# Sorted rows of an expert layer: loaded by feature blocks and transposed on VectorE, four tiles at a time, in place of TensorE transposes two tiles at a time

## The chip, the core and the metric

The kernel runs on one core of a Trainium2 chip. A core has five engines with instruction queues of their own: PE (TensorE, matmuls; its weight loads are listed as PEld), DVE (VectorE), ACT (ScalarE), POOL (GpSimd) and SP (SyncE, which here only issues DMAs). Sixteen DMA engines move the data that the queues ask for. SBUF is the on-chip memory with 128 partitions, PSUM the memory that PE writes. The metric is device time in microseconds (us) of one execution, the median of several.

## The reference

The input `x` has the shape (4, 32, 128, 128), float32, and goes through two layers.

```
# layer 0, for each of 4 batches: 128 channels-and-phases of a 64x64 image as q (128 x 4096) ... 
energy = einsum('bci,bcj->bij', q, q)            # 4096 x 4096
attn   = softmax(energy / (d_i * d_j), axis=-1)  # d = sqrt of the diagonal
x      = gamma * einsum('bcj,bij->bci', q, attn) + x
# layer 1, on tokens t of 128 features
t = t + linear_attention(layernorm(t))           # 8 heads, K'V form
n = layernorm(t)
p = softmax(n @ router_w + router_b)             # 8 experts
t = t + sum over the two likeliest experts of  p_k / (p_1 + p_2) * (n @ expert_w[k] + expert_b[k])
```

The change lies in the last line: every token goes through two of eight 128x128 expert matrices.

## The kernel before

**The long part.** For each of the four batches, PE computes the 4096 x 4096 energies by blocks of 128 x 512 (`pe`, L609), ACT takes their exponential (`pr`, L612), and PE multiplies that with q (`po`, L497). The energies are symmetric, so only half of them are computed. For the other half DVE transposes each `pr` by 32x32 pieces into a tile `F` (L421); four steps fill one `F`. SP stores `F` to DRAM (`blocks`, L530), waits for that to land, and brings it back with the 32-row groups swapped, in six DMAs (L545). PE then multiplies `F` with q (`pg`, L433), some steps later (`LAG`), ACT sums its rows (L438), and DVE adds the result (`o`, L442). One step is one `pe`, one `po` and one `pg` of 512 columns; a float32 matmul of this kind has two records in the profile.

**The second layer beside it.** For batches 0 to 2 the second layer of a batch runs in the steps of the next batch. It is written as Python generators (`layer1`, `close_rows`, `attention_rows`, `sorted_experts`), and a loop around them advances the generators as the long part goes on, so the order of instructions on PE, DVE, ACT and SP is the order in which the generators yield. Batch 3 comes last, has no long part to hide beside, and computes all experts for all tokens without sorting.

**Sorted experts.** A batch has 32 tiles of 128 tokens, handled in two halves `h`. For a half, `sorted_experts` works out a place for each of its two uses of a token, so that tokens of the same expert lie together and each expert begins at a multiple of 128 rows: `NT` = 39 tiles of 128 rows. A row has `DW` = 132 floats: 128 features and, four times, the factor that the expert's result is multiplied with. POOL scatters the rows from `xn` to the DRAM tensor `xs[h]` with indirect DMAs (L1053). Then come the sorted tiles, in pairs:

- `load` (L1083) brings two tiles from `xs[h]` into one of six buffers inside `xn`, 132 floats a row;
- three pairs later, `products` lets PE transpose the pair (L1124, two 128x128 transposes with the identity), and ACT copies the result from PSUM to SBUF (L1093);
- one pair later PE multiplies each turned tile with its expert's matrix (L1117), whose column in `ew_sb` is read from `begin` into a register (L1109, once for four tiles);
- DVE multiplies the result with the factor, which is column 128 of the loaded rows (L1099), and SP stores it to `ys` (L1103).

`hold` hands out one of three PSUM banks and empties it when `done` is called. Each pair takes two yields. At last POOL gathers the rows of `ys` back by token and adds them (L1165), and SP writes the output (L1159).

**Rows of the next batch.** `close_rows(kc)` ends the first layer for a quarter of a batch. Its `df` tile shares a buffer with the `results` of the sorted experts, and so the quarter kc = 0 waits until the batch before is `sorted`.

Of the kernel before, what the change touches and what calls it, by code (L numbers as in the profile page):

```python
# [12 lines left out]
F32 = mybir.dt.float32  # L13
BF16 = mybir.dt.bfloat16
U32 = mybir.dt.uint32
AF = mybir.ActivationFunctionType
ALU = mybir.AluOpType
# [5 lines left out]
def kernel(  # L23
# [43 lines left out]
    nc = tc.nc  # L67
    P = 128
# [8 lines left out]
    S = 32  # L77
    NH, KQ, D = wk.shape
    E = router_w.shape[1]
# [574 lines left out]
    def layer1(b, st):  # L654
# [76 lines left out]
        def close_rows(kc):  # L731


            def missing():
                return len(st["o"]) < 2 * kc + 2 or any(
                    st["got"][c] < NCH - c - (alone and c == NCH - 1) for c in (2 * kc, 2 * kc + 1)
                )

            late_rows = alone and kc >= 2
            last_rows = alone and kc == 3  # L740

            while "exps" not in st if last_rows else missing():
                yield from idle(1)
            while b > 0 and kc == 0 and not states[b - 1].get("sorted"):
                yield from idle(1)
            den, rd = (stat.tile([P, 2 * NJ], F32, tag=nm, name=f"{nm}_{b}_{kc}") for nm in ("den", "rd"))
            nc.vector.tensor_reduce(den, st["sums"][:, ts(kc, 2 * NJ), :], AX.X, ALU.add)
            nc.vector.reciprocal(rd, den)
            wide = work.tile([P, NJ, 2, 64], F32, tag="grp", name=f"rdx_{b}_{kc}", bufs=2)
            for s in range(2):  # L750
                one = rd[:, ts(s, NJ)][:, :, None]
                nc.vector.tensor_scalar(wide[:, :, s], one.to_broadcast([P, NJ, 64]), gam, None, ALU.mult)
            df = work.tile([P, 8, HW2, 2], F32, tag="df", name=f"df_{b}_{kc}", bufs=1)

            def divide(pb):
                for s in range(2):
                    own = slice(s * 64, s * 64 + 64)
                    o = st["o"][2 * kc + s]
                    for r2 in range(2):
                        rows = slice(r2 * 64, r2 * 64 + 64)  # L760
                        nc.vector.tensor_tensor(  # L761
                            df[own].rearrange("p (a k) (h t) r -> p r a (k h) t", a=4, h=2)[:, r2],
                            o[rows].rearrange("p (a j t) -> p a j t", a=4, t=S),
                            pb[own].rearrange("p (j a t) -> p a j t", a=4, t=S),
                            ALU.mult,
                        )

            yield
            if not last_rows:
                yield  # L770
                yield
            pb, done = hold(f"pbd_{b}_{kc}", divide)
            for j in range(NJ):
                nc.tensor.transpose(pb[:, ts(j, P)], wide[:, j].rearrange("p s c -> p (s c)"), ident)
            yield
            while missing():
                yield from idle(1)
            done()
            if not late_rows:
                yield  # L780
                yield
            tk = T[:, ts(kc, 8), :]
            nc.vector.tensor_tensor(tk, tk, df.rearrange("p k w r -> p k (w r)"), ALU.add)
            bs, stats = batch_stats("a", 8 * kc, 8)
            for j in range(8):
                stats[j]()
                if j == 3:
                    yield
                    yield
            close_stats("a", 8 * kc, 8, bs)  # L790
            yield from idle(1 if late_rows else 3)
            k = 8 * kc
            normalise(range(k, k + 4), rsa, nba)
            if late_rows:
                for j in range(k + 4, k + 8):
                    nc.vector.tensor_scalar(
                        xn[:, j, :D], T[:, j, :], rsa[:, j, :], nba[:, j, :], ALU.mult, ALU.add
                    )
            yield
            if last_rows:  # L800
                keep_running(36)
                done = gram_rows([k + j // 2 + 4 * (j % 2) for j in range(8)])
                yield
                done()
                return
            done = gram_rows(range(k, k + 4))
            yield
            done()
            if not late_rows:
                normalise(range(k + 4, k + 8), rsa, nba)  # L810
            yield
            done = gram_rows(range(k + 4, k + 8))
            yield
            done()
            if alone and kc < 3:
                for g in (2 * kc, 2 * kc + 1):
                    yield
                    done = transpose_rows(g)
                    yield
                    done()  # L820
# [153 lines left out]
        def sorted_experts(h):  # L974
# [98 lines left out]
            yield from idle(3)  # L1073


            bufs = [xn[:, r0 + 2 * i : r0 + 2 * i + 2, :] for i in range(8)]
            pairs = [(g, min(2, NT - 2 * g)) for g in range((NT + 1) // 2)]

            def rows_of(dram_rows, g, n):
                return dram_rows[2 * g * P : (2 * g + n) * P, :].rearrange("(j p) d -> p j d", p=P)  # L1080

            def load(g, n):
                inst = nc.sync.dma_start(bufs[g % 6][:, :n], rows_of(xs[h], g, n))  # L1083
                wait_for(inst.ins, xs_made[h], "a tile holds tokens of any row")
                xs_read[h].append(inst.ins)

            def products(turned, applied):


                def leave(p):  # L1090
                    if turned:
                        g, n = turned
                        nc.scalar.activation(  # L1093
                            bufs[6 + g % 2][:, :n, :D], p[:, : n * P].rearrange("p (j t) -> p j t", t=P), AF.Copy
                        )
                    if applied:
                        g, n = applied
                        result = keep["results"][:, g % 4]
                        nc.vector.tensor_tensor(  # L1099
                            result[:, :n], p[:, 2 * P : 2 * P + n * D].rearrange("p (j c) -> p j c", c=D),  # L1100
                            bufs[g % 6][:, :n, D : D + 1].to_broadcast([P, n, D]), ALU.mult,
                        )
                        nc.sync.dma_start(rows_of(ys, g, n), result[:, :n])  # L1103

                p, done = hold(f"pys_{b}_{h}_{(turned or applied)[0]}", leave)
                if applied:
                    g, n = applied
                    if g % 2 == 0:
                        _, at = nc.values_load_multi_w_load_instructions(  # L1109
                            begin[0:1, h, 2 * g : min(2 * g + 4, NT)], engines=[mybir.EngineType.PE], min_val=0,  # L1110
                            max_val=(E - 1) * D,
                            skip_runtime_bounds_check_because="D times a count of at most E - 1, never negative",
                        )
                        begins[:] = at
                    weights = ew_sb.rearrange("p e c -> p (e c)")
                    for j in range(n):
                        nc.tensor.matmul(  # L1117
                            p[:, 2 * P + j * D : 2 * P + j * D + D], bufs[6 + g % 2][:, j, :D],
                            weights[:, bass.ds(begins[2 * (g % 2) + j], D)], start=True, stop=True,
                        )  # L1120
                if turned:
                    g, n = turned
                    for j in range(n):
                        nc.tensor.transpose(p[:, ts(j, P)], bufs[g % 6][:, j, :D], ident)  # L1124
                return done

            if "results" not in keep:
                keep["results"] = work.tile([P, 4, 2, D], F32, tag="df", name=f"results_{b}", bufs=1)
            done = None
            begins = []  # L1130
            for at in range(len(pairs) + 5):
                if at < len(pairs):
                    load(*pairs[at])
                if done:
                    done()
                yield
                turned, applied = (pairs[at - d] if 0 <= at - d < len(pairs) else None for d in (3, 4))
                done = products(turned, applied) if turned or applied else None
                yield
            if done:  # L1140
                done()
            if h == 1:
                st["sorted"] = True
            yield from idle(1)
# [353 lines left out]
```

## Time and profile before

| what | value |
|---|---|
| median of 3 runs | 1652.24 us (1652.22 to 1652.25) |
| the profiled execution | 1659.2 us, span 1657.4 us |
| granted TensorE clock, mean | 0.996 |
| PE busy | 1623.1 us, 98% |
| DVE busy | 917.4 us, 55% |
| ACT busy | 910.4 us, 55% |
| POOL busy | 596.2 us, 36% |
| DMA packets | 241899, 332.81 MB |
| sorted loads, first and second half of batch 0 | 571 to 636 us, 661 to 719 us |
| of batch 1 | 961 to 1024 us, 1050 to 1107 us |
| of batch 2 | 1332 to 1396 us, 1415 to 1470 us |

The span is the time from the first to the last instruction of the profiled execution; its own time is 1.8 us longer. That execution is 0.4% longer than the median, so differences are compared with differences. A group line of the profile reads: line, engine, operation, tile written and tiles read, shape, number of instructions, busy time, mean nanoseconds of one, and the idle time of the engine before them with what ended it. `SPq` is SP's queue. The sorted stages in the table run from the first to the last sorted load of a half.

### The profile page before, as it was taken

Reading aid. Unit: us, or ns where it says so; the run is one execution under the profiler, and the core shown is the slowest. Engines: PE = TensorE matmul, PEld = TensorE weight load, DVE = VectorE, ACT = ScalarE, POOL = GpSimd, SP = SyncE. Lnnn points to the kernel's source line nnn. Section 1 sums busy time; section 2 is a strip of 40 time slices with the busy share of each in tenths; the row PEclk is TensorE's granted clock in tenths of the full one; section 3 lists DMA queues with packets and bytes.
Section 4 is the critical chain, followed back from the end, with each engine's and each line's share of the span. In section 5 each row is a group of like instructions: output and inputs, shape, how many; then the busy total and the mean of one; then the engine's idle time right before and its main releaser. Section 6 shows DMA issues by size and latency. Waiting matters only on the chain.

```text
span 1657.4 us, 21471 instructions
## 1 busy us (share of the span) xinstructions
PE 1623.1 (98%) x5288; PEld 856.9 (52%) x5288; DVE 917.4 (55%) x2359; ACT 910.4 (55%) x2863; POOL 596.2 (36%) x565
## 2 busy tenths in 40 slices
PE   8999999999999999999999999999999999999987
PEld 5444544455554455555564455555565445554643
DVE  4543353567486443559378453448559533344686
ACT  3555445566575555556575455556657455555376
POOL 1000000001014531456555543346546642436166
PEclk9999999999999999999999999999999999999999
DMA  4555656665349776986778868797668877885001
GB/s 147 199 181 174 198 186 213 230 212 170 131 171 277 246 220 213 271 249 176 207 200 254 265 208 255 214 287 200 167 196 239 277 222 246 240 254 168 15 14 39
DMA packets 241899, 332.81 MB, mean 201 GB/s; under 512 B 31984, under 2 KB 168304, under 8 KB 227440
## 3 DMA queue, kind: packets, MB, share of 16 engines
q1 hardware_dynamic: 207312, 291.92, 55.5%
q0 software_dynamic: 26624, 25.58, 7.5%
q10 hardware_dynamic: 7840, 13.93, 2.8%
q8 instruction: 45, 0.74, 0.2%
q14 instruction: 78, 0.64, 0.1%
HBM read 160.78 MB, written 175.80 MB: 203 GB/s over the span
## 4 chain that ended last, share of the span: by engine, by line
PE 84%; DMA 4%; DVE 4%; SPq 3%; ACT 2%; issue 2%; another core or an unknown queue 1%; POOL 0%; ACTq 0%; DVEq 0%; POOLq 0%
PE po L497 24%; PE pe L609 23%; PE pg L433 20%; PE pys L1117 3%; DMA blocks<-F 3%; PE py L1290 3%; PE pg L453 2%; SPq L545 2%; PE pat L854 2%; PE pys L1124 2%; PE pgram L728 1%; PE ptx L701 1%; DVE df L761 1%; PE pgv L839 0%
## 5 line engine op out<-in xcount | busy, mean ns | idle before, releaser
L612 ACT ACTIVATE pr<-pe 128x512 f32<-128x512 f32 (+1 forms) x576 | 322.4, 560 | 544.0 <-PE pe L609 448.2
L497 PE MATMUL po<-pr,qT 128*128 128x512 f32 (+3 forms) x1152 | 549.6, 559 | 4.2 <-ACT o L502 3.0
L609 PE MATMUL pe<-qn,qn 128*128 128x512 f32 x896 | 459.6, 595 | 2.6 <-ACT pr L612 1.6
L433 PE MATMUL pg<-F,qT 128*128 128x512 f32 x880 | 449.7, 592 | 1.1 <-DMA F<-blocks 1.1
L421 DVE STREAM_TRANSPOSE F<-pr 128x512 f32<-128x512 f32 x440 | 305.9, 702 | 144.8 <-ACT pr L612 127.0
L497 PEld LDWEIGHTS po<-pr,qT 128*128 128x128 f32 x1152 | 215.3, 190 | 251.7 <-issue 221.2
L1165 POOL DMA_INDIRECT acc<-ys,place x128 | 203.2, 1588 | 215.8 <-ACT pr L612 140.3
L438 ACT ACTIVATE junk<-F 128x512 bf16<-128x512 f32 x440 | 273.0, 620 | 1.2 <-DMA F<-blocks 1.2
L433 PEld LDWEIGHTS pg<-F,qT 128*128 128x128 f32 x880 | 166.7, 190 | 195.4 <-issue 181.0
L1053 POOL DMA_INDIRECT xs<-xn,place x192 | 186.0, 969 | 189.7 <-ACT pr L612 116.6
L609 PEld LDWEIGHTS pe<-qn,qn 128*128 128x128 f32 x896 | 155.0, 191 | 115.0 <-issue 104.6
L442 DVE TENSOR_TENSOR o<-o,pg 128x512 f32<-128x512 f32 x110 | 75.3, 684 | 207.9 <-PE pg L433 173.4
L1099 DVE TENSOR_TENSOR results<-pys,xn 128x256 f32<-128x256 f32 x120 | 49.9, 416 | 187.1 <-ACT xn L1093 122.0
L164 POOL TENSOR_TENSOR rn<-ss,neg_half 128x8 f32<-128x8 f32 (+1 forms) x17 | 27.2, 1602 | 320.9 <-DVE ss L296 320.8
L612 ACT ACTIVATION_READ_ACCUMULATOR pr<-pe 128x1 f32 x576 | 112.0, 194 | 0.0
L1093 ACT ACTIVATE xn<-pys 128x256 f32<-128x256 f32 x120 | 45.2, 377 | 112.5 <-PE pys L1124 94.5
L1117 PEld LDWEIGHTS pys<-ew_sb,xn 128*128 128x128 f32 x468 | 70.4, 191 | 53.0 <-issue 49.5
L1165 POOL DMA_INDIRECT yb<-ys,place x64 | 61.8, 965 | 84.5 <-DMA F<-blocks 31.1
L609 PE MATMUL pe<-qn 128*128 128x512 f32 (+3 forms) x256 | 90.2, 435 | 0.7 <-ACT qn L342 0.7
L438 ACT ACTIVATION_READ_ACCUMULATOR junk<-F 128x1 f32 x440 | 84.6, 192 | 0.0
L1117 PE MATMUL pys<-ew_sb,xn 128*128 x468 | 71.7, 275 | 0.4 <-ACT xn L1093 0.4
L164 POOL TENSOR_TENSOR rsa<-dm_a,neg_half 128x8 f32<-128x8 f32 x16 | 28.9, 1807 | 103.1 <-DVE sv_a L688 102.9
(216 smaller groups left out, 1521.1 us busy)
## 6 DMA issues: line engine op xcount, KB each, us to landing
blocks<-F SPq DMA_DIRECT2D x110, 1024.0 KB
F<-blocks SPq DMA_DIRECT2D x220, 192.0 KB
F<-blocks SPq DMA_DIRECT2D x220, 128.0 KB
xn<-xs SPq DMA_DIRECT2D x114, 132.0 KB
ys<-results SPq DMA_DIRECT2D x114, 128.0 KB
F<-blocks SPq DMA_DIRECT2D x220, 64.0 KB
below<-F SPq DMA_DIRECT2D x31, 384.0 KB
T<-in_x_dram SPq DMA_DIRECT2D x64, 128.0 KB
```

Source lines behind the costliest of these rows:

```text
L164: pinned(nc.gpsimd.tensor_tensor(dst, src, neg_half.to_broadcast(list(src.shape)), ALU.pow))
L421: f()
L433: nc.tensor.matmul(pg.rearrange("p (a f) -> p a f", a=4), st["qT"][i][:, ib, :], G[:, :, ib], start=(ib == 0), stop=(ib == NJ - 1),)
L438: nc.scalar.activation(junk, G[:, :, ib], AF.Copy, accum_out=st["sums"][:, NJ * i + ib, jc : jc + 1])
L442: nc.vector.tensor_tensor(st["o"][jc], st["o"][jc], pg, ALU.add)
L497: nc.tensor.matmul(row["po"][:, lo:hi], qT[blk // NJ][:, blk % NJ, :], w, start=start, stop=(row["left"] == 0))
L609: nc.tensor.matmul(pe[:, c0:], qn[jc][:, ts(j, P)], qn[i][:, c0:], start=True, stop=True)
L612: nc.scalar.activation(pr[:, c0:], pe[:, c0:], AF.Exp, accum_out=sums[:, t, i : i + 1]).ins
L1053: inst = nc.gpsimd.indirect_dma_start(xs[h], offset(place[:, i, k : k + 1]), xn[:, k, :], None)
L1099: nc.vector.tensor_tensor(result[:, :n], p[:, 2 * P : 2 * P + n * D].rearrange("p (j c) -> p j c", c=D), bufs[g % 6][:, :n, D : D + 1].to_ ...
L1117: nc.tensor.matmul(p[:, 2 * P + j * D : 2 * P + j * D + D], bufs[6 + g % 2][:, j, :D], weights[:, bass.ds(begins[2 * (g % 2) + j], D)], st ...
L1165: inst = nc.gpsimd.indirect_dma_start(to, None, ys, offset(place[:, i, k : k + 1]), compute_op=op)
```

## The change

Sorted tiles are handled in fours (`quads`, ten for each half, the last with three tiles) and turned without PE and ACT.

- `load` issues four DMAs, one for each block of 32 features. Block `q` goes to partitions 32q to 32q+31: partition 32q+i receives, for each group m of 32 rows, the 32 features of row 32m+i. Each piece is 128 bytes long. The two load buffers, and two for turned tiles, lie in this half's part of `xn`.
- `turn` is one DVE instruction: it transposes every 32x32 piece of the 128x512 tile, which leaves features on partitions and rows along the free axis.
- `product` multiplies four tiles into one PSUM bank; its `leave` multiplies 128x512 at once with `factor` and stores four tiles with one DMA.
- `factor` is a tile of 128x39, loaded once for a half by one DMA that picks column 128 of every row, 4 bytes at a time.
- One quad is loaded every four yields; its turn is due eight yields later, its product eleven, and its result thirteen.
- `close_rows` of all quarters waits until the batch before is `sorted`; a quarter also waits until the quarter two before it has been added, and, before it takes a PSUM bank, until the one before it has.

```diff
-            while b > 0 and kc == 0 and not states[b - 1].get("sorted"):
+            added = st.setdefault("added", set())
+            while b > 0 and not states[b - 1].get("sorted") or kc > 1 and kc - 2 not in added:
                 yield from idle(1)
...
+            while kc > 0 and kc - 1 not in added:
+                yield
             pb, done = hold(f"pbd_{b}_{kc}", divide)
...
             nc.vector.tensor_tensor(tk, tk, df.rearrange("p k w r -> p k (w r)"), ALU.add)
+            added.add(kc)
...
-            bufs = [xn[:, r0 + 2 * i : r0 + 2 * i + 2, :] for i in range(8)]
-            pairs = [(g, min(2, NT - 2 * g)) for g in range((NT + 1) // 2)]
...
-                inst = nc.sync.dma_start(bufs[g % 6][:, :n], rows_of(xs[h], g, n))
...
-                        nc.scalar.activation(
-                            bufs[6 + g % 2][:, :n, :D], p[:, : n * P].rearrange("p (j t) -> p j t", t=P), AF.Copy
-                        )
...
-                        nc.tensor.transpose(p[:, ts(j, P)], bufs[g % 6][:, j, :D], ident)
...
+            room = xn[:, half, :].rearrange("p k w -> p (k w)")
+            parts = [room[:, 4 * DW * i : 4 * DW * i + 4 * D] for i in range(4)]
+            quads = [(g, min(4, NT - 4 * g)) for g in range((NT + 3) // 4)]
+            factor = stat.tile([P, NT, 1], F32, tag="factor", name=f"factor_{b}_{h}")
...
+            def load(g, n):
+                rows = xs[h][4 * g * P : (4 * g + n) * P, :D].rearrange("(m i) w -> i m w", i=S)
+                for q in range(4):
+                    read(
+                        nc.sync.dma_start(
+                            parts[g % 2][ts(q, S), : n * D].rearrange("i (m c) -> i m c", c=S), rows[:, :, ts(q, S)]
+                        )
+                    )
+
+            def turn(g, n):
+                nc.vector.transpose(parts[2 + g % 2][:, : n * D], parts[g % 2][:, : n * D])
+
+            def product(g, n):
 
                 def leave(p):
+                    result = keep["results"][:, ts(g % 2, 4)]
+                    nc.vector.tensor_tensor(
+                        result[:, :n], p[:, : n * D].rearrange("p (j c) -> p j c", c=D),
+                        factor[:, 4 * g : 4 * g + n].to_broadcast([P, n, D]), ALU.mult,
+                    )
...
+                for j in range(n):
+                    nc.tensor.matmul(
+                        p[:, ts(j, D)], parts[2 + g % 2][:, ts(j, D)],
+                        weights[:, bass.ds(begins[j], D)], start=True, stop=True,
+                    )
...
+            read(nc.sync.dma_start(factor, xs[h].rearrange("(t p) w -> p t w", p=P)[:, :, D : D + 1]))
+            leaves = {}
+            for at in range(4 * len(quads) + 10):
+                for first_at, act in ((8, turn), (0, load), (11, product), (13, lambda g, n: leaves.pop(g)())):
+                    if at >= first_at and (at - first_at) % 4 == 0 and (at - first_at) // 4 < len(quads):
...
+                yield
```

## The prediction

> **What bounds the kernel now.** I read the page's busy shares first, then the PE groups with their idle time, the instructions of PE in order of time inside one sorted stage, the DMA share by stage, and last SP's waits.
>
> The page says that PE (TensorE's matmuls) is busy nearly all the time, at an undiminished clock:
>
> ```profile
> span 1657.4 us, 21471 instructions
> PE 1623.1 (98%) x5288; PEld 856.9 (52%) x5288; DVE 917.4 (55%) x2359; ACT 910.4 (55%) x2863; POOL 596.2 (36%) x565
> ...
> PEclk9999999999999999999999999999999999999999
> DMA  4555656665349776986778868797668877885001
> ```
>
> The PE groups show who makes PE wait. The number after the bar is busy time, then the mean of one, then idle time before:
>
> ```profile
> L433 PE MATMUL pg<-F,qT 128*128 128x512 f32 x880 | 449.7, 592 | 1.1 <-DMA F<-blocks 1.1
> L1117 PE MATMUL pys<-ew_sb,xn 128*128 x468 | 71.7, 275 | 0.4 <-ACT xn L1093 0.4
> L1124 PE MATMUL pys<-ident,xn 128*128 128x128 f32 x234 | 45.1, 273 | 0.0
> ```
>
> All idle time before PE instructions adds up to 26 us, most of it at the start and after 1500 us. The reader is to see that in the sorted stages PE works through its list without a hole, so a matmul taken off the list there shortens the run by the room it took, as long as everything that feeds PE keeps pace. That room is not the mean duration. In order of time:
>
> ```profile
> 642.53 0.61 PE L1117 MATMUL pys<-ew_sb,xn 128*128 x4
> 642.98 0.38 PE L1124 MATMUL pys<-ident,xn 128*128 128x128 f32 x2
> 643.20 0.81 PE L609 MATMUL pe<-qn 128*128 128x384 f32 x2
> ```
>
> Two transposes start at 642.98 and the next matmul at 643.20: 0.11 us each. Over all 234 of L1124 the distance to the next start adds up to 25.5 us, 0.109 each.
>
> What feeds PE is the DMA round trip of F (L530 out, L545 back, used by L433). These are the six stages with sorted loads, two for each of batches 0 to 2; the last two numbers are DMA share and GB/s:
>
> ```profile
> 571.00:636.00 65.00, 64.82 (x223) 34.50 (x222) 29.31 (x52) 34.39 (x106) 27.54 (x30) 1.00 0.75 229
> 661.00:719.00 58.00, 58.00 (x215) 32.38 (x214) 27.38 (x52) 30.05 (x93) 28.10 (x18) 1.00 0.95 254
> 961.00:1024.00 63.00, 62.82 (x218) 33.66 (x217) 28.72 (x52) 33.15 (x101) 26.95 (x29) 1.00 0.74 232
> 1050.00:1107.00 57.00, 57.00 (x213) 31.76 (x212) 27.38 (x52) 29.36 (x90) 27.59 (x18) 1.00 0.98 257
> 1332.00:1396.00 64.00, 62.46 (x222) 34.02 (x222) 22.82 (x45) 34.02 (x107) 26.20 (x29) 1.00 0.77 243
> 1415.00:1470.00 55.00, 55.00 (x209) 31.41 (x208) 24.30 (x48) 29.64 (x92) 30.42 (x32) 1.00 0.85 253
> ```
>
> The first stage of a batch leaves the DMA engines a quarter of their time, the second hardly any. The share adds up packet times, which overlap a little: its highest stretch of 10 us anywhere is 1.14, which I take as full. From packet records and PE starts I worked out how early F is back: 9 to 14 us before PE needs it in the first stages, 5 to 11 in the second. That slack is what the change can use up.
>
> **The change, part by part.**
>
> *Transposes off PE.* 117 pairs of tiles, 234 transposes, gone: 234 x 0.109 = 25.5 us. The 468 records of L1117 (two for each of 234 products) and one register load for each four tiles stay. The Trainium skill ("TensorE: Matmul & The Clock Gate", Part 4) gives about 275 ns for a transpose inside a kernel; the mean record here agrees (273 ns), but starts lie 109 ns apart, and by 275 the gain would be 64 us. I go by the distance of starts.
>
> *Copies off ACT.* 120 of L1093, 45.2 us. ACT is 55% busy and mostly waits for PE, so nothing is gained or lost.
>
> *DVE.* 60 turns of 128x512 at L421's 0.70 us add 42 us; 60 multiplies of 128x512 at L442's 0.68 replace 120 of L1099 at 0.416, 41 against 50. Net 33 us, 5.6 in a stage where DVE is busy 23 to 29 of 55 to 65 us. Its idle time covers it; without that, 33 us.
>
> *SP.* 240 loads and 6 factor columns replace 120 loads, 60 stores replace 120: 66 more issues, at 0.43 us 28 us, under 5 a stage. SP is occupied 52 to 73% of the stages, so this fits.
>
> *New waits.* Load g on SP waits for turn g-2 on DVE, listed just ahead of it; behind it queue F's stores and returns. SP already waits there for DVE:
>
> ```profile
> SPq L545 <- DMA blocks<-F: 215.2, 64, 6.1
> SPq L1103 <- DVE results L1099: 79.9, 38, 9.2
> ```
>
> so it is paced by DVE now, and half of the L1103 waits go. A turn waits on DVE for a load listed four steps earlier, some 12 us. Loads now land 1.5 to 6 us after issue, plus 1.3 for three more issues, so it is normally there. Late, it would hold F's transposes (L421) behind it. I cost both at 0 to 2 us a stage, 1 where DMA is tight.
>
> *Order of rows.* close_rows moves one `pbd` by two or three matmuls and one `pgram` past a `pbd`, in batches 1 and 2; the tail of batch 3 has the old order. Nothing.
>
> *DMA, the open price.* Half a batch has 39 tiles. Before: 4992 packets of 528 bytes, taking 9.3 us of 16 engines together (mean 31.9 ns). After: 19968 of 128 bytes, and 4992 of 4 bytes for the factor column. The trace has no 128-byte packet. Its nearest rows, median time of a packet: 9 ns at 4 and 32 bytes, 27 at 512, 84 at 2048, 311 at 8192, which lie on 8.2 ns + 0.037 a byte. That line puts 128 bytes at 13 ns. From below the bound is 9, from above 27, if small reads are served no faster than 512-byte ones. Net per half:
> - 13 ns (factor 9): 16.2 + 2.8 - 9.3 = +9.7 us
> - 15 ns: +12
> - 18 ns for the rows: +16
> - 22 ns for both: 27.5 + 6.9 - 9.3 = +25
> - 27 ns for both: 33.7 + 8.4 - 9.3 = +33
>
> A stage shrinks by 4 us (25.5/6). What does not fit into 1.14 of the rest, beyond a slack of 9 us (first stages) or 5.5 (second), PE waits for. Second stages hold 55.1, 55.9 and 46.8 us of DMA work (share by length) and have room for 61.3, 60.2 and 57.9 (1.14 x 53.8, 52.8, 50.8). At 15 ns the first two overflow by 5.8 and 7.7, so 0.3 + 2.2, rounded up to 3 us of waiting; at 18 by 9.8 and 11.7, so 10.5; at 22 all three, 13.3 + 15.2 + 8.4 = 37. At 27: second stages 21 + 23 + 16, first stages (48.8 + 33 against 69.3, less 9) some 4 each, 73 us. First stages cost nothing up to 22. I take 15 ns, close to the line, with 2 added because the pieces lie 528 bytes apart, at uneven addresses, which no row prices.
>
> The Trainium skill speaks against the change: "DMA: Bandwidth & Descriptors" (Specifications) wants at least 512 bytes for line rate. Read as "128 bytes cost what 512 do", it gives the 27 ns sum below, 1700. No row here settles it.
>
> **Sum.** -25.5 (PE) + 3 (DMA) + 2 (new waits) = -20 us. The profiled execution took 1659.2 us (span 1657.4 and 1.8 around it), 0.4% above the 1652.2 median, so it becomes 1639, and the median 1632.
>
> **Rivals.**
> *A: the DMA engines become the bound (slower).* Mechanism: 128-byte reads cost as much as 512-byte ones, the queue that also carries F fills in the second stages, and L433 waits for F. It decides from about 20 ns on, where the waiting equals 25.5 us. At 22 ns: 1652 - 25.5 + 37 = 1664; at 27: 1652 - 25.5 + 73 = 1700. For it: shares of 0.95 and 0.98, and the one place where DMA backs up today (L433, 1.1 us, at 184 us, as large set-up transfers run) shows that F can arrive late. Against it: the straight line of packet times.
> *B: the wait moves to DVE or SP.* Turns late behind their loads, or the 4992 single elements of the factor column block the queue at the head of a stage. The column takes 2.8 to 8.4 us of the queue a half (9 and 27 ns each). At 2 us of stall in each of six stages 12 us go: 1639; with the column at 8.4, 3 us over the slack in three stages, 21 go: 1648. Against it: the slack, and turns that come 12 us behind their loads.
> *C: the freed room isn't used, no change.* PE would have to wait for ACT or DVE by the same amount; both are half idle, so hardly.
>
> **How the numbers follow.** Forecast (1626 to 1638) 0.42; B 0.11; A 0.44; C 0.03. Forecast and B are faster, A is slower. The range takes the forecast and B whole and A up to 22 to 27 ns: 1626 to 1690, leaving out the dearest part of A and a gain above the 25.5 us. Measurement can tell about 0.2%, 3.3 us. Faster 0.53, same 0.03, slower 0.44.
>
> **What would show it.** Right: L1124 and L1093 gone, PE's busy time near 1598, 128-byte packets at 13 to 15 ns, idle time before L433 a few us, DMA share in second stages about 1.1. Wrong: idle before L433 or L497 of tens of us at 660 to 730 and 1050 to 1120 with releaser F (A), or idle before L421 or the turn released by a load, and SP waiting for turns (B). Wrong in size: PE idle for ACT.

## The result, and the profile after

| kernel | median | ratio to before, 95% interval |
|---|---|---|
| before | 1652.23 us | |
| changed | 1657.99 us (1656.07 to 1660.49, 6 runs) | 1.0041 [1.003, 1.0051] |
| changed, in a later comparison (f0) | 1660.80 us | 1.0054 [1.0038, 1.0071] |

The changed kernel is 0.4 to 0.5% slower, some 7 to 9 us by the ratios, where 20 us of gain were forecast. The chips of the comparisons differ by up to 10 us (the kernel before took 1649.82 on one and 1660.19 on another), so every ratio is to runs of the kernel before on the same chip. For a comparison place by place I use a trace of the unchanged kernel taken with the experiments (e0, span 1651.0 us).

The page of the changed kernel (profiled execution 1658.15 us):

```profile
span 1655.8 us, 20777 instructions
...
PE 1604.1 (97%) x5054; PEld 832.1 (50%) x5054; DVE 944.1 (57%) x2359; ACT 869.0 (52%) x2743; POOL 591.3 (36%) x565
...
DMA  5554756665359898996768789797567999996001
```

PE lost 234 instructions and 19 us of busy time, but the span did not follow. PE waits now, 43.9 us in all against 21.9 in e0. The waits of PE (us in total, times, the longest), in the changed kernel:

```profile
PE pg L433 <- DMA F<-blocks: 7.6, 6, 2.4
PE pgram L728 <- DVE gram L722: 5.7, 2, 2.9
PE pys L1121 <- DVE xn L1099: 5.7, 4, 2.0
```

L433 is F back late, the first line that the forecast watched. The wait of `pys` (the sorted product) begins with a DMA as well; for `gram` that is argued here, and e3 shows it for a part. The groups of DVE (the last columns are idle time and what ended it) show the turn waiting for its load, and the first layer's `df` waiting for a store of the expert results that share its buffer:

```profile
L762 DVE TENSOR_TENSOR df<-o,pbd 64x512 f32<-64x512 f32 x64 | 43.9, 686 | 21.9 <-PE pbd L777 10.8 <-DMA ys<-results 10.4
...
L1099 DVE STREAM_TRANSPOSE xn<-xn 128x512 f32<-128x512 f32 (+1 forms) x60 | 40.6, 677 | 60.2 <-DMA xn<-xs 60.0
```

**Where.** Set matching matmuls of the changed kernel and e0 side by side by their order. The changed kernel is 8.5 us ahead when its PE reaches 667 us (2.9 of them from before any sorted load, so no part of the change), and 0.8 at 767. It gains some 6 until 1064 and loses some 13 until 1167, gains some 6 until 1431 and loses some 5 until 1525. The gains are the first halves and what lies around them. The losses are the second halves and, behind the first two of them, `close_rows`. The first two second halves by windows (length, then busy time of PE, PEld, DVE, ACT, POOL, then granted clock, DMA share, GB/s), first in the changed kernel, then in e0, and last the second window in e2, a variant told below that loads 512-byte pieces and keeps the gain:

```profile
647.00:719.00 72.00, 68.04 (x217) 34.58 (x216) 36.91 (x62) 30.63 (x95) 30.95 (x20) 1.00 0.96 216
1037.00:1111.00 74.00, 69.25 (x214) 34.79 (x213) 37.41 (x62) 30.58 (x95) 29.84 (x20) 0.98 0.94 212
```

```profile
647.00:719.00 72.00, 71.82 (x255) 39.17 (x254) 32.47 (x63) 37.75 (x117) 27.31 (x18) 1.00 0.89 242
1037.00:1111.00 74.00, 73.82 (x264) 40.31 (x263) 32.62 (x62) 38.16 (x119) 29.09 (x19) 1.00 0.89 244
```

```profile
1037.00:1111.00 74.00, 73.23 (x238) 37.79 (x237) 41.75 (x76) 32.41 (x102) 38.17 (x25) 1.00 1.02 264
```

PE idles 4 to 5 us in each window of the changed kernel. Its DMA engines are somewhat busier than in the same windows of e0 (0.96 and 0.94 against 0.89) and move less. But e2 has them at 1.02 and 264 GB/s while PE hardly waits, so it isn't their capacity that ended.

**Each wait costs twice.** PE in order of time at one of the late F, and the granted clock (PEclk) of four stretches behind waits of 2.0 to 2.9 us:

```profile
1084.52 1.02 PE L497 MATMUL po<-pr,qT 128*128 128x512 f32 x2
1087.93 1.10 PE L433 MATMUL pg<-F,qT 128*128 128x512 f32 x2 [2.39 <-DMA F<-blocks]
1088.87 1.84 PE L609 MATMUL pe<-qn,qn 128*128 128x512 f32 x2
1090.50 1.92 PE L497 MATMUL po<-pr,qT 128*128 128x512 f32 x2
1092.21 1.09 PE L433 MATMUL pg<-F,qT 128*128 128x512 f32 x2
```

```profile
761.20:764.60 3.40, 3.40 (x8) 1.80 (x8) 3.31 (x5) 0.99 (x3) 2.91 (x3) 0.51 0.11 22
1088.90:1092.30 3.40, 3.40 (x6) 1.34 (x5) 0.97 (x2) 1.30 (x4) 0.60 (x1) 0.50 1.13 246
1153.80:1160.60 6.80, 5.62 (x13) 3.56 (x14) 6.63 (x13) 1.84 (x6) 5.08 (x4) 0.50 0.46 117
1471.20:1474.60 3.40, 3.40 (x8) 1.72 (x7) 2.96 (x5) 0.69 (x2) 0.00 (x0) 0.50 0.84 242
```

The pairs at 1088.87 and 1090.50 take 1.84 and 1.92 us, and start 1.6 to 1.7 us apart instead of 0.86. Four such stretches, 17 us in all, cost up to 8.5 us on top of the waits. e0 has none between 30 and 1570 us.

**SP.** DMA-issuing instructions don't count as busy, so the page has no line for them. Adding up the durations of all DMA instructions on SP's queue gives 722 us in e0 (1541 of them) and 813 in the changed kernel (1607). In order of time, first the unchanged kernel (e0), then the changed one, each across a few us of batch 0's second half:

```profile
685.95 0.42 SPq L1083 DMA_DIRECT2D xn<-xs  x1
686.47 0.41 SPq L1103 DMA_DIRECT2D ys<-results  x1
686.98 0.42 SPq L1083 DMA_DIRECT2D xn<-xs  x1
687.49 0.49 SPq L1103 DMA_DIRECT2D ys<-results  x1
```

```profile
683.40 2.69 SPq L1093 DMA_DIRECT2D xn<-xs  x4
686.19 1.88 SPq L1109 DMA_DIRECT2D ys<-results  x1
688.17 2.31 SPq L1093 DMA_DIRECT2D xn<-xs  x4
690.58 2.86 SPq L545 DMA_DIRECT2D F<-blocks  x6
693.54 0.38 SPq L1109 DMA_DIRECT2D ys<-results  x1
693.96 0.50 SPq L530 DMA_DIRECT2D blocks<-F  x1
694.56 3.89 SPq L1093 DMA_DIRECT2D xn<-xs  x4
```

The second column is the duration. Four loads hold the queue for 2.3 to 3.9 us, a store behind them for 1.88, and F's return (L545) and store (L530) stand behind both.

How much of F's lateness arises there can be read by matching packet records, in order, to F's stores and returns. In the second halves, from F's fourth transpose (L421) to its landing, 19.3 us pass in e0 and 27.1 in the changed kernel, in the mean. F's time in flight (its store, and its last return, each from issue to landing) did not grow: 7.9 and 7.6 us. All else, time in which F stands in SP's queue, went from 11.3 to 19.5. The largest part of it, from the transpose to the issue of F's store, went from 6.5 to 11.7 us, and the time that SP spends in it issuing other DMAs from 4.3 to 8.4.

### The profile page after: what moved, and what is told of

Read it like the earlier page. It is cut to its first block, busy times and chain, and to the rows that moved or that the text cites. A ratio compares the mean times of both kernels' runs of the same rounds, so it can differ in the third digit from the quotient of the medians.

```text
span 1655.8 us, 20777 instructions
## 1 busy us (share of the span) xinstructions
PE 1604.1 (97%) x5054; PEld 832.1 (50%) x5054; DVE 944.1 (57%) x2359; ACT 869.0 (52%) x2743; POOL 591.3 (36%) x565
## 4 chain that ended last, share of the span: by engine, by line
PE 78%; DMA 8%; DVE 6%; SPq 3%; issue 2%; ACT 2%; POOL 1%; ACTq 0%; DVEq 0%; POOLq 0%
PE po L497 23%; PE pe L609 22%; PE pg L433 19%; PE py L1287 3%; PE pys L1121 2%; PE pg L453 2%; PE pgram L728 2%; PE pat L858 2%; DMA F<-blocks 1%; DMA blocks<-F 1%; DMA acc<-ys,place 1%; DMA xn<-xs 1%; SPq L545 1%; DMA acc<-t 1%; DMA ys<-results 1%
## 5 line engine op out<-in xcount | busy, mean ns | idle before, releaser
L433 PE MATMUL pg<-F,qT 128*128 128x512 f32 x880 | 450.3, 593 | 8.1 <-DMA F<-blocks 7.6
L421 DVE STREAM_TRANSPOSE F<-pr 128x512 f32<-128x512 f32 x440 | 303.8, 698 | 176.4 <-ACT pr L612 166.1
L433 PEld LDWEIGHTS pg<-F,qT 128*128 128x128 f32 x880 | 166.7, 191 | 206.2 <-issue 179.4
L609 PEld LDWEIGHTS pe<-qn,qn 128*128 128x128 f32 x896 | 159.5, 191 | 134.8 <-issue 129.0
L1121 PEld LDWEIGHTS pys<-ew_sb,xn 128*128 128x128 f32 x468 | 61.4, 192 | 32.7 <-issue 23.9
L1099 DVE STREAM_TRANSPOSE xn<-xn 128x512 f32<-128x512 f32 (+1 forms) x60 | 40.6, 677 | 60.2 <-DMA xn<-xs 60.0
L1121 PE MATMUL pys<-ew_sb,xn 128*128 x468 | 62.5, 276 | 5.7 <-DVE xn L1099 5.7
L1287 PE MATMUL py<-ew_sb,xn 128*128 128x512 f32 x128 | 60.2, 610 | 5.1 <-ACT tmp L1244 3.9
```

Of the source, the lines that this page charges most:

```text
L421: f()
L433: nc.tensor.matmul(pg.rearrange("p (a f) -> p a f", a=4), st["qT"][i][:, ib, :], G[:, :, ib], start=(ib == 0), stop=(ib == NJ - 1),)
L609: nc.tensor.matmul(pe[:, c0:], qn[jc][:, ts(j, P)], qn[i][:, c0:], start=True, stop=True)
L1121: nc.tensor.matmul(p[:, ts(j, D)], parts[2 + g % 2][:, ts(j, D)], weights[:, bass.ds(begins[j], D)], start=True, stop=True,)
L1287: nc.tensor.matmul(bank, xn[:, k, :D], ew_sb[:, 4 * h : 4 * h + 4, :], start=True, stop=True)
```

## The experiments

Two theories were left by the comparison. *Pieces*: the many 128-byte packets fill the DMA engines. *Queue*: what SP has to issue fills SP's in-order queue, and F's stores and returns, loads and stores all come late. With them went two smaller suspects, the buffer shared by `df` and `results`, and the factor column.

**e0_before: the kernel before, unchanged.**

> The kernel before, unchanged, profiled again beside the others. Both theories: 1652 us, so a ratio of 1.000 to the runs of before. Its profile tells whether the 7 us by which the first profiled execution (1659.2 us) lay over its median belong to that execution: if the profile lies at 1652 again, the two traces may not be compared by their totals, only place by place.

0.9999 [0.999, 1.0009]. A difference of a tenth of a per cent is about what a comparison leaves open.

**e1_no_turn: what the transposes are worth.** In the kernel before, the transposes and copies are left out, so that the product takes the loaded rows as they are.

```diff
-  p[:, 2 * P + j * D : 2 * P + j * D + D], bufs[6 + g % 2][:, j, :D],
+  p[:, 2 * P + j * D : 2 * P + j * D + D], bufs[g % 6][:, j, :D],
...
-  turned, applied = (pairs[at - d] if 0 <= at - d < len(pairs) else None for d in (3, 4))
+  turned, applied = None, (pairs[at - 4] if 0 <= at - 4 < len(pairs) else None)
```

> The kernel before without its transposes on TensorE and without the copies on ScalarE: the product takes the loaded rows as they are (this part of the computation is left out). Loads, stores and VectorE work are those of before. If the 25.5 us that the prediction gave for the transposes are right, 1627 us (ratio 0.9846). Rival, something else than TensorE's list sets the end of the sorted stages: 1640 us or more.

1631.01 us, 0.9879 [0.9863, 0.9894]: 20 us. PE's 25.5 us are there to be had, less some 4 us more of waiting (idle 25.5 against 21.9).

**e2_wide_rows: the changed kernel with one load for four tiles, in 512-byte pieces.** The turn is issued all the same, but on rows so loaded it doesn't transpose a whole tile; this order of data is what is left out.

```diff
-  for q in range(4): ... parts[g % 2][ts(q, S), : n * D] ... rows[:, :, ts(q, S)]
+  read(nc.sync.dma_start(parts[g % 2][:, : n * D].rearrange("p (j d) -> p j d", d=D),
+      xs[h][4 * g * P : (4 * g + n) * P, :D].rearrange("(j p) d -> p j d", p=P)))
```

> The changed kernel, but each quad is loaded by one DMA with pieces of 512 bytes, row by row, so that the turn on VectorE no longer yields the true transpose (the order of the data is left out). Theory 1, the number of pieces delays F and the stores in the second stages: the waits of TensorE for F vanish, 1637 us or less. Theory 2, the loss comes from close_rows waiting for the last store of the results in the shared buffer: still 1648 us or more. If both hold, between.

1630.13 us, 0.9883 [0.9866, 0.99]. Turns on DVE, products by four, factor column, the new order of `close_rows` and the shared buffer are all in it, and it keeps 19 us of gain. So the loss hangs on how the rows are loaded. PE's and DVE's waits in this kernel:

```profile
PE pg L433 <- DMA F<-blocks: 1.9, 2, 1.1
...
PE pgram L728 <- DVE gram L722: 1.5, 2, 1.0
```

```profile
DVE xn L1098 <- DMA xn<-xs: 21.6, 11, 5.4
```

Even so its second halves have become tight. Between F's landing and PE's need of it, packet records and PE starts of the first two batches leave 1.6 to 5.4 us there (and nothing for one F, at 1075 us), against 5.4 to 10.7 in e0: enough for PE but for that one, and little is left.

**e3_own_results: results of the second half in a free part of `xn`, not in df's buffer**.

```diff
-  result = keep["results"][:, ts(g % 2, 4)]
+  result = results[:, ts(g % 2, 4)]   # h == 1: in xn[:, :HR]
```

> The changed kernel with the results of the second half in a part of xn that is free by then, so that df of the next batch no longer waits for the last stores of the second half. Theory 1 (pieces): no more than 5 us better, 1653 us. Theory 2 (the shared buffer): VectorE no longer waits 4.1 and 6.3 us for the store, TensorE does not wait for gram, and 5.3 + 8.6 = 14 us come back, 1644 us.

1652.18 us, 1.0014 [1.0005, 1.0024], some 4 to 7 us better than the changed kernel (1.0041 and 1.0054). `df` no longer waits for a store (10.4 us before); PE's wait for `gram` goes from 5.7 to 3.4 us. The shared buffer is a part of the loss, not its main cause.

**e4_all_partitions and e5_plain_factor: other forms of the same packets.** e4 gives each of the four loads all 128 partitions and one tile, in 128-byte pieces. e5 reads the factor tile in 156-byte pieces instead of 4992 single elements.

```diff
-  parts[g % 2][ts(q, S), : n * D].rearrange("i (m c) -> i m c", c=S), rows[:, :, ts(q, S)]
+  parts[g % 2][:, : n * D].rearrange("p (q j c) -> p q j c", q=4, c=S)[:, :, j], rows   # e4
-  factor, xs[h].rearrange("(t p) w -> p t w", p=P)[:, :, D : D + 1]
+  factor.rearrange("p t w -> p (t w)"), xs[h][:P, :NT]                                  # e5
```

> The changed kernel with the same number of DMAs and of 128-byte pieces, but each DMA brings one tile to all 128 partitions instead of four tiles to 32 (so the blocks lie in another order and the turn isn't the true transpose). Theory 1a, the number of small pieces costs the time: as the changed kernel, 1658 us. Theory 1b, four DMAs that write to only 32 partitions each are what is slow: near the wide rows' 1630 us.

> The changed kernel, but the factor tile is loaded in pieces of 156 bytes, one for each partition, instead of 4992 pieces of 4 bytes (its values are left out). If the column counts by its packets' time (9 ns each, 2.8 us of 16 engines a half), some 3 us in each second stage come back: 1648 to 1652 us. If single elements are dearer than their records say, more: 1640 us.

e4 1.0066 [1.0052, 1.008], e5 1.0100 [1.0086, 1.0114]. e4 came near its theory 1a, e5 missed both of its numbers. Neither gains: the number of partitions isn't it, nor are the single elements. That e5 is slower than the changed kernel isn't explained. Its profiled run has waits of 10.4 us at 1450 and 7.2 us at 1527 that the changed kernel's traces don't have; e4 and e6, from the same chip, have waits of 4 to 11 us near them too.

**e6_more_time: e2 with four more DMAs per quad, DRAM to DRAM, 128 rows of 512 bytes each.**

```diff
+  for m in range(4):
+      inst = nc.sync.dma_start(spare[g % 2][ts(m, k), :], xs[h][4 * g * P + m * k : 4 * g * P + (m + 1) * k, :D])
```

> The wide rows (1630 us) with four more DMAs for each quad, issued with the load, which copy the same rows from DRAM to a spare DRAM tile in pieces of 512 bytes: 4992 more packets a half, at 27 ns 8.4 us of 16 engines, so that the DMA time for each quad is that of the changed kernel's 19968 packets of 14 ns. Theory 1c, it is the DMA engines' time whatever the size of the pieces: back to 1650 to 1658 us. Theory 1d, the number of descriptors is what costs, beyond their recorded time: 1640 us or less.

1697.88 us, 1.0231 [1.0211, 1.0251], far beyond both numbers. It adds packets and issues together, so it tells the theories apart only with f3.

**e7_first_halves: the new way in the first half of a batch, the old one in the second**.

```diff
+  yield from (new_way if h == 0 else old_way)()
```

> The new way in the first half of each batch, the old one in the second; the result is complete. If the losses belong to the second stages and what follows them, the three first stages keep their 4.2 us each and the rest is as before: 1652 - 12.7 = 1639 us, plus or minus 3. If new small reads cost wherever they run, 1646 us or more.

1651.45 us where before took 1659.79: 0.9946 [0.9932, 0.9959], some 9 us of gain, between the two numbers expected. By the ratios it is faster than both kernels, and its result is complete.

**f0_after: the changed kernel again.**

> [...] All theories: ratio 1.004 as on the first chip, up to 1.010 on a chip where the kernel before is slower too.

1.0054, as shown above; SP's issues take 809 us.

**f1_deep_second: second half with four load buffers and the turn twelve yields behind its load**, results in `xn`.

```diff
-  for first_at, act in ((8, turn), (0, load), (11, product), ...
+  for first_at, act in ((12, turn), (0, load), (15, product), ...   # h == 1, four load buffers
```

> The changed kernel, but in the second half of a batch four load buffers instead of two (the first half's part of xn is free by then), the turn twelve yields behind its load instead of eight, and the results there too instead of in the buffer that df takes over. The DMAs are the same. Theory A, turns that wait for late loads hold VectorE, and with it F: VectorE's 60 us of waits for loads fall below 25, and the second stages keep their gain: 12 us better than the changed kernel or more. Theory B, the DMA engines are full whatever the order: the waits move to F, and no more than 6 us are won (the results' buffer alone brought about 6).

1667.02 us, 1.0095 [1.0077, 1.0114], a miss. What theory A asked for came: VectorE's waits at the turn for loads fell from 60.0 us to almost none. The gain didn't. VectorE now waited for the stores of the results instead, and PE's wait for turns grew to 11.3 us:

```profile
DVE xn L1106 <- DMA ys<-xn: 58.3, 17, 6.3
```

F's store left SP some 17 us after its last transpose in batch 0's second half, against 12 in the changed kernel: loading earlier didn't make the queue less late. Why the stores of the results come later stays open.

**f2_act_queue: the row loads issued by ACT, one yield later**.

```diff
-  nc.sync.dma_start(
+  nc.scalar.dma_start(
```

> The changed kernel with its row loads issued from ScalarE's queue, one yield later, so that F's stores and returns no longer stand behind them in one ring of each DMA engine. Theory A (order): F returns earlier, 8 us better than the changed kernel or more, less what ScalarE loses by issuing 240 DMAs at 0.45 us. Theory B (full engines): within 4 us of it.

1654.29 us, 1.0028 [1.0013, 1.0043], some 4 us better than f0, at the edge of theory B. SP's issues fall to 640 us, the turn's wait for its load to 7.6 us, and F's lateness to 2.0 us. But ACT, which makes `pr` for PE, issues 240 DMAs of 0.52 us, and the price moves there:

```profile
PE pe L609 <- ACT pr L612: 11.6, 7, 3.4
PE pgram L728 <- DVE gram L722: 5.7, 2, 2.9
...
PE pg L433 <- DMA F<-blocks: 2.0, 3, 1.1
```

**f3_more_issues: e2 with three small DMAs more per quad, 16 rows of 512 bytes each**, so that SP issues as many DMAs as in the changed kernel.

```diff
+  for m in range(3):
+      inst = nc.sync.dma_start(spare[g % 2][ts(m, 16), :], xs[h][4 * g * P + 16 * m : 4 * g * P + 16 * m + 16, :D])
```

> The wide rows with three small DMAs more for each quad (16 rows of 512 bytes each, DRAM to DRAM), so that SyncE issues as many DMAs as in the changed kernel, with a tenth of the packets added. If the number of issues on SyncE costs, 1645 us or more; if the DMA engines' time does, as the wide rows: ratio 0.988 to 0.992.

1657.56 us, 1.0038 [1.0024, 1.0052], with 2880 packets more than e2. All of the gain is gone, place by place as in the changed kernel. The added DMAs take 0.73 us each on SP and bring its sum from 685 to 816 us. The DMA engines are less busy than in e2 and in e0 (0.86 and 0.83 in the two windows above), and F, with 26.3 us from transpose to landing, is nearly as late as in the changed kernel. This run parts the queue from the DMA engines.

**g1_one_issue and g2_four_issues: pieces and DMAs apart.** g1 loads 2048 pieces of 128 bytes by one DMA; g2 loads 512 of 512 bytes by four (one for each tile).

```diff
+  rows = xs[h][start : start + 4 * n * P, :S].rearrange("(m p) c -> p m c", p=P)                        # g1
+  read(nc.sync.dma_start(parts[g % 2][:, : n * D].rearrange("p (m c) -> p m c", c=S), rows))
+  for j in range(n):                                                                                     # g2
+      read(nc.sync.dma_start(parts[g % 2][:, ts(j, D)], xs[h][(4 * g + j) * P : (4 * g + j + 1) * P, :D]))
```

> The changed kernel, with the 2048 pieces of 128 bytes of four tiles loaded by one DMA to 128 partitions instead of four DMAs to 32 each. The pieces lie 528 bytes apart as before, but are the first 32 features of 2048 rows, so the rows that reach the product are not those of the tiles (the data's order is left out). Packets per quad as in the changed kernel, DMAs on SP's queue 3 fewer per quad (180 fewer in all, at 0.69 us each in the trace). Theory Q (the length of SP's queue costs the time: F's stores and returns stand in it behind the loads): the ratio falls to 0.985 to 0.991, like that of the one-DMA load of whole rows (0.9883), and F's waits before L433 are under 3 us. Theory P (many small packets on the DMA engines cost the time): 1.002 to 1.006, like the changed kernel (1.0041, 1.0054).

> The changed kernel, with four tiles loaded by four DMAs in pieces of 512 bytes, one tile each (the turn then does not transpose a whole tile: the order of data is left out). A quarter of the packets, as many DMAs on SP's queue as in the changed kernel. Theory Q: 1.000 to 1.006, PE idle 38 us or more, half-clock periods in the sorted stages. Theory P: 0.985 to 0.991, as with one DMA per four tiles.

Neither theory's numbers came; both were half right. Ratios, and in brackets the sum of SP's issues:

| | one DMA for a quad | four DMAs |
|---|---|---|
| 512-byte pieces | 0.9883 [0.9866, 0.99] (685 us, e2) | 0.9976 [0.9966, 0.9986] (779 us, g2) |
| 128-byte pieces | 0.9984 [0.9975, 0.9993] (795 us, g1) | 1.0041 [1.003, 1.0051] (813 us, changed) |

At 1650 us to the whole, the pieces alone cost 17 us, the DMAs alone 15, both together 26. How small pieces cost without more DMAs is seen on SP, first e2, then g1, at corresponding places of batch 1's second half:

```profile
1081.02 0.38 SPq L1091 DMA_DIRECT2D xn<-xs  x1
1082.56 0.34 SPq L530 DMA_DIRECT2D blocks<-F  x1
1083.00 1.61 SPq L1108 DMA_DIRECT2D ys<-results  x1
```

```profile
1084.02 0.36 SPq L1092 DMA_DIRECT2D xn<-xs  x1
1084.48 4.50 SPq L1105 DMA_DIRECT2D ys<-results  x1
1089.27 2.83 SPq L545 DMA_DIRECT2D F<-blocks  x3
```

The load of 2048 pieces is off the queue in 0.36 us, but the next DMA takes 4.50 to issue, and F's return waits behind that. The DMA issued next after a load takes 2.24 us in the mean of all 60 loads in g1, 0.54 in e2. Over all 60 stores the mean is 1.44 us in g1, 0.51 in e2, at a median of 0.38 in both. The pieces are paid for in SP's queue as well. The Trainium skill ("DMA: Bandwidth & Descriptors", "Anatomy of one DMA") calls descriptor generation small, with many descriptors to be had before a cost shows. Its table is for DMAs that POOL issues; on SP's queue here 2048 of them showed, as 4.50 us in the next issue.

**g3_two_queues: two of the four loads of the second half on ACT, results of that half in `xn`**.

```diff
+  for q in range(2, 4):
+      load_part(nc.scalar, rows, g, n, q)   # h == 1, one yield later
```

> The changed kernel's whole computation; in the second half of each batch two of the four row loads of a quad are issued by ACT, one step later, the other two by SP, and the results of that half stand in the free part of xn instead of df's buffer. Theory Q: 20 fewer issues of 0.69 us on SP in a second stage, 14 us, and 10 us more on ACT, half of what made PE wait for pr (11.6 us) when ACT issued all four; with the df wait gone too (two stalls of 2.9 us and half a clock behind them), 0.990 to 0.997. Theory P: the packets are the same, so only the df wait goes, 1.000 to 1.003.

1659.86 us, 1.0058 [1.0045, 1.0071], a miss. SP's sum fell to 771 us and `df`'s wait went, yet F's lateness doubled to 14.5 us and turns wait 79.3 us for loads. The loads on ACT come one yield later, and a quad is complete only when both queues have issued their part; which of the two it is, no run separates. What they do to SP can be seen: from F's last transpose to its store 15.4 us pass, and SP issues for 8.4 of them, as in the changed kernel, but stands waiting itself for 7.0 (3.2 there). So the sum of SP's issues isn't a price list: it orders the load forms e2, g2, g1 and the changed kernel, not this one, nor e3, whose 809 us go with 1.0014, nor e5, whose 783 go with 1.0100.

**g4_first_halves_again: e7 once more.**

> The version with the new way in the first half of each batch and the old one in the second, once more. By the traces the first sorted stages keep 13 us of PE room (three of 4.3 us) and the second ones lose nothing against before: 0.992 to 0.996 again, if nothing in it hangs on the chip that it ran on.

1653.01 us where before took 1660.19: 0.9937 [0.9912, 0.9961]. F's waits before L433 are down to 0.9 us in e7, and no clock stretch lies in a second half. With the old way there alone, the gain stays: the losses belong to the second halves, and this is the version to keep.

## Why the prediction was wrong

**Right: the transposes.** 25.5 us by distances of starts; e1 and e2 gain 20 and 19 us with some 4 us of new waiting.

**Right: the packet's price.** 119808 packets of 128 bytes have a median of 13 ns and a mean of 14.3. All DMA work grew by 58 us of sixteen engines (1103 to 1161), 9.6 a half, where the straight line gave 9.7 and the sum took 12. (The 9.3 us in it is a slip: 4992 packets of 31.9 ns are 10.0 us of sixteen engines, so the line gives 9.0.) The trace decides against reading the skill's 512-byte rule as "128 bytes cost what 512 do": that was 27 ns.

**Wrong: the capacity that ended.** The step "What does not fit into 1.14 of the rest, beyond a slack of 9 us (first stages) or 5.5 (second), PE waits for" took the DMA engines for the thing that fills, with 1.14, the highest share of any 10 us, as full. The second halves stood at 0.94 and 0.96 as wholes while PE waited, where e2 ran at 1.02 with its gain kept and f3 lost all of it at 0.83 and 0.86. F's time in flight did not grow. So the 3 us that the sum gives to DMA have nothing behind them.

**Wrong: the step that failed, SP.** "66 more issues, at 0.43 us 28 us ... so this fits." They took 91 us more (813 against 722): the 240 loads 166.4 us, 0.69 each, against 69.1 for 120; the 60 stores 32.8 against 63.3; the column 2.7; and some 21 us are DMAs that the change doesn't touch. The 0.43 was the mean of F's returns (L545); the loads of before, the nearer row, already took 0.57, and a load of 512 short pieces has another form again. And occupancy was the wrong measure: in an in-order queue what SP issues ahead of F goes onto F's round trip, in a stage with 5 us to spare. From transpose to landing F took 27.1 us in the second halves instead of 19.3, all of it added in SP's queue. In the second halves of batches 0 and 1 this left F 0.6 to 4 us, or none. f3 and g2 show the DMAs' part, g1 the pieces'.

**Wrong in size: the new waits, 2 us.** The queue's delay came back at three places, not one: F (7.6 us), turns late behind loads (5.7 on PE, 60.0 on DVE), and `df` behind a store (5.7 at `pgram`). "Order of rows ... Nothing" missed that `df` shares its buffer with `results` and that the last store stands behind `out_dram` on SP; e3 prices it at some 4 to 7 us. And a wait was costed at its length; half a clock for 3.4 us behind it adds up to 1.7.

**The rivals.** A had the sign and the place (L433, second halves), but not the mechanism: packets were below its 20 ns. That 1658 lies inside 1626 to 1690 is luck, since only A's price reaches so far and that price didn't come. B had the mechanism of late turns but at most 21 us of loss, which kept it faster. Its factor column costs little: 2.7 us of issues in all, with 3 to 4 us in the load behind it in four of the six halves, but not in those where batches 0 and 1 lose (0.33 there). C didn't come.

**Why it isn't slower still.** The first halves keep 7 to 14 us of slack for F, and there the queue's delay is hidden; e7 and g4 keep their gain.

**What stays open.** By idle time (22 us more than e0) and half clocks (some 4 us more, counting e0's own before 30 and after 1570 us), the changed kernel's loss comes to some 26 of the 30 us between -25.5 and the +4.8 of the spans; the rest I did not place. Nor do the runs show why many pieces lengthen an issue on SP: in the issue itself, or because the DMA engines take the pieces up slowly.

## What to carry to other kernels

Price a DMA by what it holds on its queue as well as by its packets: take the duration of the issuing instruction and of the one behind it, for the shape that the change will have, and ask what stands behind it in that queue. Where an engine waits for a round trip through the same queue, the round trip's slack is the budget, stage by stage; a change can gain in a stage with 10 us of slack and lose more in one with 5, and the two may be built differently.

## What the runs showed of the hardware

- **Half a clock after short waits.** In the changed kernel PE waits of 2.0, 2.4, 2.9 and 1.0 + 2.9 us were followed by 3.4 us (6.8 after the last) at half the granted clock. Its waits up to 1.5 us were not, but in e3 one of 1.6 us was (at 1434). Nor was each longer one: 2.1 us at 697 in this kernel, 2.7 us at 698 in g1 and 3.2 us at 1075 in f2 had none. The Trainium skill ("TensorE: Matmul & The Clock Gate", Part 1) tells of a free-running window of about 3.4 us after which an idle PE is throttled; that fits stretches of 3.41 us and the chance in it. Its advice to avoid gaps of over 3 us (same page, "Why this matters for your kernels") is too generous here, where 1.6 us were enough.
- **A DMA's pieces are paid for by the next one's issue**: 4.50 us behind a DMA of 2048 pieces that itself took 0.36, 2.24 in the mean of 60 (g1), 0.54 behind 512 pieces (e2).
